# Regrouped weight loads and a moved row-moment step in a graph-attention kernel with fast matrix products

## The chip, the cores and the metric

The kernel runs on one core of one Trainium2 chip. The metric is the device time of one execution in microseconds. Before the change three runs gave a median of 3197.68 us (3193.69 to 3199.67). One execution was also recorded by the hardware profiler; all profile lines come from that one.

The names of the engines: PE is the matrix engine (PEld its weight loads), DVE the vector engine, ACT the scalar engine, POOL the GpSimd engine, SP the sync engine, whose queue (SPq) issues nearly all DMA transfers. Each engine runs its own instructions in order; engines wait for each other by semaphores.

## The reference

One attention layer over 128 graphs of 128 nodes, width 768, 12 heads of 64, all in float32:

```python
h = jnp.maximum(_layernorm(x, axis=-1), 0.0)
q = _split_heads(h @ Wq + bq); k = _split_heads(h @ Wk + bk); v = _split_heads(h @ Wv + bv)
scores = jnp.einsum('bhqd,bhkd->bhqk', q, k) / sqrt(64)
scores = jnp.where(adj > 0, scores + beta * adj, -9e15)
out = x + concat_heads(jnp.einsum('bhqk,bhkd->bhqd', softmax(scores), v))
```

x is (128, 128, 768), adj is (128, 128, 128) with some 12% of its entries above zero, and each of the three weight matrices is (768, 768), 2.36 MB.

## The kernel before, in words

Four graphs make a group `G` (512 rows); there are 32 groups. For each group the projections are done in three slices of equal size: `qk0` (the first half of the columns of q and k), `v`, and `qk1` (the second half of q and k). A slice is a matrix product of blocks, activations `A{r}{k}` by weights `B{k}{j}`, and is computed by a scheme of 15 block products instead of 18 (`PRODUCTS`): some factors are sums of activation blocks (`SUMS_A`, on DVE by `sum_acts`), some are sums of weight blocks (`SUMS_B`). In the slices `qk0` and `v` each of the 15 products is itself done by 7 products of quarters instead of 8 (`product_z`, line 486); that needs four more sums of each activation factor (`inner`, on POOL, L422 to L425, kept in the tiles `SP`), seven prepared quarters of each weight factor (`prepare`, made once at the start and kept in DRAM as `kept_qk` and `kept_v`), and a decoding on POOL (`decode`). The prepared weight tiles `T` of 448 KB are read back for each group by `load_T` (L301) into a ring of five (`RING`); the same five tiles serve `prepare` at the start. Each product issues the load of the tile five products later. The slice `qk1` uses plain products (`product`, L575) with its weights held on chip.

The first group is different: its `qk0` and `v` slices are plain (`plain_slice`, L780), and meanwhile `prepare` makes the 30 weight tiles from the raw weights: DVE makes the sums (L223, L225), POOL the quarters (L250 to L253, L276 to L279), SP sends the tile to DRAM (L255, L281). Group 1's statistics (`stats` L325, `moments_1` L336) stand inside group 0's `v` slice, on PE at its seventh product. The raw weights are loaded block by block by `load_weights`: `load_part` (L195) takes a block of 256 input rows in two DMAs of 128 rows each, and the DRAM side of such a DMA is a pattern of 4 by 32 rows (the kernel keeps its input rows in an order in which 32 neighbours lie together). The first three blocks are issued from SP and ACT, the rest from SP. The raw `qk0` and `v` blocks lie in the tiles that later hold `SP` (and, for the last three, `xo`), the `qk1` blocks in tiles of their own. SP's order at the start is: x of two graphs, first weights, x of the other two, the other `qk0` weights, adjacency and bias, `v` weights, `qk1` weights, first kept tile, x of group 1 (L165), the other kept tiles.

For groups from 3 on, the statistics of a group's rows are taken two groups ahead from copies of x (`load_halves` L370, `row_stats` L378), in the `qk1` slice. `row_moments` turns them into scale and shift: two instructions on DVE (L385, L387), two on POOL (L389, L390), then a small store to DRAM and a load back that spreads them over the partitions (L393, L394). `add_raw` loads the group's adjacency by four DMAs (L432); `bias_steps` turns it on DVE (L440) and makes the mask from it.

Attention is woven in between: `scores` (L613, L617, L620) for three heads pairs at a time, then `attend` places eight small steps between matrix products (`turn`). At the end of four of them `weigh` takes the row sums on DVE (L627, L628, L630) and ACT divides (L634). The result is added to x on POOL (`add`, L661) and stored (`send`, L664).

Inside the main loop the order of every engine's work is the order in which the program writes it. `run` (L748) is what writes it: for each product it issues the first half (matrix products, and the attention steps between them), then the functions that `todo` holds for this product (the fillers), then what `later` has put off for this product (`overdue`), then the second half (evacuation and accumulation of the product), then the functions held for "post". The steps of the change are in this order: in the loop over `G`, `row_moments` and `add_raw` for group `G + 1` are fillers of product 0 of the `qk0` slice.

Of the kernel before, what the change touches and what calls it, by code (L numbers as in the profile page):

```python
# [10 lines left out]
F32 = mybir.dt.float32  # L11
# [6 lines left out]
P = 128  # L18
HEADS = 12
GRP = 4  # L20
# [77 lines left out]

AS_SUMMED = ("B01", "B12", "B02", "B22", "B10", "B00", "B21", "B20", "B11")
SLICES = ("qk0", "v", "qk1")  # L100

# [15 lines left out]
def direct(ctx, tc, x, adj, wq, bq, wk, bk, wv, bv, beta, out, bad):  # L117
# [10 lines left out]
    nc = tc.nc  # L128
# [62 lines left out]

    def load_part(w, k, at, n, t, engine):
        src = w.rearrange("(a c j) n -> c a j n", a=NB, j=SQ)
        for c in range(2):
            engine.dma_start(t[:, c], src[2 * k + c][:, :, at:at + n])  # L195

    def load_block(sl, k, j, t, engines):
        if sl == "v":
            load_part(wv, k, j * 2 * P, 2 * P, t, engines[0])
        else:  # L200
            for i, w in enumerate((wq, wk)):
                load_part(w, k, (j + 3 * int(sl[2])) * P, P, t[:, :, i * P:(i + 1) * P], engines[i % len(engines)])

    nraw = [0]

    def load_weights(sl, blocks=[f"B{k}{j}" for j in range(3) for k in range(3)], engines=(nc.sync,)):
        for b in blocks:
            if sl == "qk1":
                t = const.tile([P, 2, H2], F32, name=f"{sl}_{HOME.get(b, b)}")
            else:  # L210
                n = nraw[0]
                nraw[0] += 1
                if n < len(PRODUCTS):
                    t = work.tile([P, GRP, P], F32, tag=f"SP{n}", name=f"{sl}_{b}", bufs=1)
                else:
                    t = work.tile([P, GRP, P], F32, tag="xo", name=f"{sl}_{b}", bufs=3)
                t = t.rearrange("p (c i) n -> p c (i n)", c=2)
            load_block(sl, int(b[1]), int(b[2]), t, engines)
            wt[sl, b] = t

# [6 lines left out]
    def sum_weights(sl, n):  # L227
        name, a, b, sign = SUMS_B[n]
        if (sl, name) not in wt:
            raw = [r for r, home in HOME.items() if home == name]  # L230
            wt[sl, name] = wt[sl, raw[0]] if raw else const.tile([P, 2, H2], F32, name=f"{sl}_{name}")
        sum_to(nc.vector, wt[sl, name], wt[sl, a.strip("-")], a[0] == "-", wt[sl, b], sign)
# [7 lines left out]
    def prepare(sl):  # L240

        def home(n):
            return work.tile([P, 7, P], F32, tag="T", name=f"prep_{sl}_{n}", bufs=RING)

        def whole(b):
            return wt[sl, b].rearrange("p c (i n) -> p c i n", i=2)

# [11 lines left out]
        def sums(name):  # L259
            for out, a, b, sign in SUMS_B:  # L260
                if out == name:
                    if out not in made:
                        made[out] = home(int(out[1:]))
                    at = [quarters(made[q]) if q in made else whole(q) for q in (a.strip("-"), b)]
                    sum_to(nc.vector, quarters(made[out]), at[0], a[0] == "-", at[1], sign)

        def finish(name):
            n = [i for i, p in enumerate(PRODUCTS) if p[1] == name][0]
            if name in made:
                rest(n, made[name])  # L270
            else:
                t, b = home(n), whole(name)
# [3 lines left out]
                e.tensor_tensor(t[:, 2], b[:, 1, 1], b[:, 0, 1], ALU.subtract)  # L276
# [141 lines left out]
    def inner(G, n):  # L418
        a = A[G, PRODUCTS[n][0]]
        t = SP[G, n] = work.tile([P, GRP, P], F32, tag=f"SP{ZORDER.index(n)}", name=f"SP{n}_{G}", bufs=1)  # L420
        e = nc.gpsimd
        e.tensor_tensor(t[:, 0], a[:, 0, N:H2], a[:, 1, N:H2], ALU.add)  # L422
# [33 lines left out]

    between, deferred = deque(), deque()

# [103 lines left out]
    def product(G, sl, n, order):  # L562
# [8 lines left out]
        for i in range(2):  # L571
            for c in range(2):
                lhs, rhs = b[:, c, i * P:(i + 1) * P], a[:, c, :]
# [67 lines left out]
    def attend_steps(G, oc):  # L641
        o = work.tile([P, 2, 4, HD], F32, tag="o", name=f"o_{G}_{oc}", bufs=2)
        for r in range(2):
            bank = take()
            pa = bank[:, 0:4 * VE].rearrange("p (b e) -> p b e", e=VE)
            for g in range(2):
                for i in range(2):
# [17 lines left out]

        later(add)
        later(send, 2)
        yield True
# [95 lines left out]
    def plain_slice(G, sl, todo):  # L764

        n = 0
        for r in range(2):
            for j in range(3):
# [4 lines left out]
                for at, k in [(at, k) for at in parts for k in range(3)]:  # L773
                    a, b = A[G, f"A{r}{k}"], wt[sl, f"B{k}{j}"]
                    for i in range(2):
                        for c in range(2):
                            lhs, rhs = b[:, c, i * P:(i + 1) * P], a[:, c, at]
                            if sl == "v":
                                lhs, rhs = a[:, c, i * N:(i + 1) * N], b[:, c, :]
                            last = nc.tensor.matmul(p[:, i, at], lhs, rhs, start=(k == 0 and i == 0 and c == 0),  # L780
# [170 lines left out]

    load_weights("qk1", AS_SUMMED)
    prep = deque(prepare("qk0") + prepare("v"))
# [44 lines left out]
    for G in range(1, NG):  # L998
# [41 lines left out]
        if G + 2 < NG:  # L1040
# [161 lines left out]
```

## Time and profile before

| | |
|---|---|
| median of 3 runs | 3197.68 us |
| the profiled execution | 3211.7 us, of which 3209.8 us span |
| mean granted clock of PE | 0.946 |
| busy: PE, DVE, ACT, POOL | 88%, 67%, 42%, 73% |
| DMA | 660.85 MB, mean 206 GB/s |
| one middle group | about 96.5 us |

The profile page lists busy time by engine, and then groups of instructions: line and engine, operation, output<-input by the program's names, partitions x elements, count, busy us, mean ns of one, and the idle time of the engine just before them with what ended it. A time line has one row for each run of equal instructions: start and duration in us, engine, line, operation, count, and in brackets the idle time before it and what ended that. For SPq the duration is that of issuing, with what it waited for between issues of one row. The waits list who waited for whom, with the total in us, the number of times and the longest. Windows give busy us of each engine in a stretch of time, then PE's granted clock, the mean busy share of the 16 DMA engines, and GB/s.

In a middle group the three slices stand at, for example, 983.5 to 1023.5 (`qk0`), 1023.5 to 1050.7 (`v`) and 1050.7 to about 1080 us (`qk1`); PE is busy 31.18 of 40.00 us, 26.56 of 27.20 and 29.30 of 29.30 in them.

### The profile page before, as it was taken

The numbers are of one execution on the slowest core, as the hardware profiler recorded it, in microseconds if no ns is written. First come the engines' busy times: TensorE is split into PE (matmuls) and PEld (weight loads), VectorE is DVE, ScalarE is ACT, GpSimd is POOL, SyncE is SP. The second block draws the span as 40 slices with busy tenths as digits, with TensorE's granted clock in tenths as the row PEclk, the third lists the DMA queues.
The fourth block names the chain that finished last, engine by engine and source line by source line (L and its number), as shares of the span: only waits on it lengthen the run. The fifth ranks groups of instructions, "written<-read, shape, count | busy, mean of one in ns | idle before, by whom it ended". The sixth has DMA issues, their size and how long they took to land.

```text
span 3209.8 us, 113028 instructions
## 1 busy us (share of the span) xinstructions
PE 2830.4 (88%) x46385; PEld 2462.4 (77%) x46385; DVE 2155.4 (67%) x4755; ACT 1338.4 (42%) x3999; POOL 2331.3 (73%) x4146
## 2 busy tenths in 40 slices
PE   7379988889888889888889888889888889888898
PEld 5267787778787778787778787778887778787787
DVE  3367666667666667667667667667666667666665
ACT  1134344344344344444344445344444344445343
POOL 2578677878777878767878677878777778677784
PEclk9689999999999999999999999999999999999999
DMA  3566776767776767776667776767776667776654
GB/s 95 172 184 186 235 227 206 207 196 215 233 225 206 207 193 211 237 221 201 205 195 221 238 221 202 206 195 218 239 230 203 201 194 217 237 222 202 199 186 146
DMA packets 531311, 660.85 MB, mean 206 GB/s; under 512 B 105181, under 2 KB 407529, under 8 KB 530793
## 3 DMA queue, kind: packets, MB, share of 16 engines
q1 hardware_dynamic: 529672, 652.81, 67.6%
q8 instruction: 367, 6.01, 0.8%
q14 instruction: 152, 1.24, 0.1%
q10 hardware_dynamic: 1120, 0.79, 0.1%
HBM read 589.26 MB, written 64.21 MB: 204 GB/s over the span
## 4 chain that ended last, share of the span: by engine, by line


## 5 line engine op out<-in xcount | busy, mean ns | idle before, releaser
L499 PE MATMUL bank<-SP,T_qk 128*64 128x128 f32 x7440 | 718.4, 287 | 0.2 <-issue 0.2
L499 PE MATMUL bank<-S,T_qk 128*64 128x128 f32 x4092 | 453.5, 295 | 255.2 <-DMA T_qk<-kept_qk 159.5
L499 PE MATMUL bank<-T_v,SP 128*64 128x128 f32 x7440 | 647.7, 273 | 0.0
L634 ACT ACTIVATE o<-bank,sm 128x64 f32<-128x64 f32 x1524 | 353.4, 315 | 679.0 <-DVE sm L628 583.6
L650 PEld LDWEIGHTS bank<-v,e 128*64 128x64 f32 x6048 | 427.2, 137 | 108.4 <-issue 1.0
L499 PEld LDWEIGHTS bank<-S,T_qk 128*64 128x64 f32 x4092 | 287.8, 150 | 279.3 <-DVE qk L526 136.8
L499 PEld LDWEIGHTS bank<-SP,T_qk 128*64 128x64 f32 x7440 | 496.5, 147 | 0.5 <-issue 0.5
L499 PEld LDWEIGHTS bank<-T_v,SP 128*64 128x64 f32 x7440 | 460.0, 137 | 0.0
L650 PE MATMUL bank<-v,e 128*64 128x65 f32 x6048 | 446.1, 221 | 0.9 <-issue 0.9
L575 PE MATMUL bank<-S,qk_T 128*64 128x256 f32 x3584 | 445.0, 381 | 0.0
L499 PE MATMUL bank<-T_v,S 128*64 128x128 f32 x4092 | 405.7, 274 | 18.8 <-ACT v L513 14.8
L585 ACT ACTIVATE qk<-bank,bqk 128x256 f32<-128x256 f32 x384 | 158.4, 475 | 569.5 <-PE bank L575 431.2
L544 POOL TENSOR_TENSOR qk<-qk 128x256 f32<-128x256 f32 x186 | 135.6, 729 | 357.2 <-DVE qk L525 357.2
L525 DVE TENSOR_TENSOR v<-v,bank 128x512 f32<-128x512 f32 x310 | 212.0, 684 | 156.9 <-PE bank L499 94.5
L575 PEld LDWEIGHTS bank<-S,qk_T 128*64 128x64 f32 x3584 | 235.5, 138 | 81.5 <-issue 2.2
L499 PEld LDWEIGHTS bank<-T_v,S 128*64 128x64 f32 x4092 | 260.1, 137 | 33.5 <-ACT v L513 23.9
L555 POOL TENSOR_TENSOR v<-v 128x128 f32<-128x128 f32 x186 | 85.5, 460 | 266.4 <-DVE v L525 172.1
L575 PE MATMUL bank<-S,qk_B 128*64 128x256 f32 x2048 | 276.0, 380 | 0.0
L525 DVE TENSOR_TENSOR qk<-qk,bank 128x512 f32<-128x512 f32 x310 | 209.3, 675 | 98.7 <-PE bank L499 97.4
L661 POOL TENSOR_TENSOR xo<-xo,o 128x512 f32<-128x512 f32 x189 | 254.6, 1347 | 11.7 <-ACT o L634 11.7
L617 DVE SCALAR_TENSOR_TENSOR e<-bank,biasT 128x512 f32<-128x512 f32 x378 | 236.5, 681 | 28.1 <-PE bank L613 27.0
L575 PE MATMUL bank<-A,qk_T 128*64 128x256 f32 x2048 | 249.1, 379 | 0.0
(157 smaller groups left out, 5882.5 us busy)
## 6 DMA issues: line engine op xcount, KB each, us to landing
T_qk<-kept_qk SPq DMA_DIRECT2D x465, 448.0 KB
T_v<-kept_v SPq DMA_DIRECT2D x465, 448.0 KB
x<-in_x_dram SPq DMA_DIRECT2D x254, 192.0 KB
xo<-in_x_dram SPq DMA_DIRECT2D x189, 256.0 KB
out_dram<-xo SPq DMA_DIRECT2D x189, 256.0 KB
half<-in_x_dram SPq DMA_DIRECT2D x232, 192.0 KB
adj<-in_adj_dram SPq DMA_DIRECT2D x128, 64.0 KB
kept_qk<-prep_qk SPq DMA_DIRECT2D x15, 448.0 KB
```

Source lines behind the costliest of these rows:

```text
L499: nc.tensor.matmul(p[z // 4][q:q + HD, z % 4, :], lhs[:, q:q + HD], rhs, start=(first and z % 4 == 0), stop=True, skip_group_check=True)
L525: nc.vector.tensor_tensor(t[:, 0:4], t[:, 0:4], p[0], op)
L544: e.tensor_tensor(t[:, 1:4:2], t[:, 1:4:2], twice(0), ALU.add)
L555: e.tensor_tensor(v[:, 0:2, 0:HD], heads(0), heads(3), ALU.add)
L575: nc.tensor.matmul(p[q:q + HD, i, :], lhs[:, q:q + HD], rhs, start=(first and i == 0 and c == 0), stop=(c == 1), skip_group_check=True)
L585: opened[0] = nc.scalar.activation(t[:, i, :], p[:, i, :], AF.Identity, bias=bqk[:, i, oc:oc + 1], scale=float(sign))
L617: taken[0] = nc.vector.scalar_tensor_tensor(e, ps[oc, i].rearrange("p (g n) -> p g n", g=GRP), SCORE_CAP * ISCALE, biasT[G], op0=ALU.min, ...
L634: nc.scalar.activation(o[:, b], pa[:, b, 0:HD], AF.Copy, scale=t[:, 1, b:b + 1])
L650: nc.tensor.matmul(pa[q:q + HD, 2 * g + i, :], es[G, oc, i][:, 2 * r + g, q:q + HD], vt[G, "v", r, h // 4][:, 4 * g + h % 4, :], start=Tru ...
L661: nc.gpsimd.tensor_add(t, t, o.rearrange("p a (b j) d -> p (a b) (j d)", j=2))
```

## The change

Four things are done at once.

Weights: the raw weights of a slice are loaded into one large tile. A DMA takes 32 input rows (one value of `a`) with all six chunks of rows (`c`) and 128 to 512 columns; q and k of `qk0` in two parts (first column block, then the other two), `v` in one part of 512 columns and three small tiles for the last 256, `qk1` in one part. All are issued from SP. The blocks `B{k}{j}` are views of the large tiles.

Sums: the 15 `SP` tiles become slots of one tile, `spbuf`, which also holds the raw `qk0` and `v` weights at the start. Because of it the first group's DVE order differs: its 11 activation sums stand ahead of the first weight sums, where they alternated.

Moments and adjacency: `row_moments` and `add_raw` move from product 0 of a group's `qk0` slice to product 14 of the `qk1` slice before it, behind the other fillers there.

Row sums: `weigh` and the release of its bank are put off until the fillers of the same product have been issued (`weighing`); the add and the store of an attention result move one product later.

The lines of the profile of the changed kernel are shifted by 2 or 3, for example L393 becomes L395 and L301 becomes L303.

```diff
-    def load_part(w, k, at, n, t, engine):
-        src = w.rearrange("(a c j) n -> c a j n", a=NB, j=SQ)
-        for c in range(2):
-            engine.dma_start(t[:, c], src[2 * k + c][:, :, at:at + n])
...
+    spbuf = const.tile([P, len(PRODUCTS), GRP, P], F32, name="spbuf")
+    rows_of = {}
+    for name, w in (("q", wq), ("k", wk), ("v", wv)):
+        rows_of[name] = w.rearrange("(a c j) n -> a j c n", a=NB, j=SQ)
+
+    def load_cols(engine, t, name, at, chunks=slice(0, NC)):
+        for a in range(NB):
+            engine.dma_start(t[a * SQ:(a + 1) * SQ], rows_of[name][a][:, chunks, at:at + t.shape[-1]])
+
+    def flat(lo, hi):
+        return spbuf[:, lo:hi].rearrange("p s g n -> p (s g n)")
+
+    def raw_qk(u, t, parts):
+
+        v = t.rearrange("p (c i j n) -> p c i j n", c=NC, i=2, j=3)
+        for lo, hi in parts:
+            for i, name in enumerate(("q", "k")):
+                load_cols(nc.sync, v[:, :, i, lo:hi].rearrange("p c j n -> p c (j n)"), name, (lo + 3 * u) * P)
+        for k in range(3):
+            for j in range(3):
+                wt[f"qk{u}", f"B{k}{j}"] = v[:, 2 * k:2 * k + 2, :, j]
+
+    def raw_v():
+        t = flat(9, 15).rearrange("p (c n) -> p c n", c=NC)
+        load_cols(nc.sync, t, "v", 0)
+        for k in range(3):
+            own = work.tile([P, GRP, P], F32, tag="xo", name=f"v_B{k}2", bufs=3)
+            own = own.rearrange("p (c i) n -> p c (i n)", c=2)
+            load_cols(nc.sync, own, "v", 4 * P, slice(2 * k, 2 * k + 2))
+            for j in range(3):
+                b = t[:, 2 * k:2 * k + 2, j * 2 * P:(j + 1) * 2 * P] if j < 2 else own
+                wt["v", f"B{k}{j}"] = b.rearrange("p c (i n) -> p c i n", i=2)
...
-    load_weights("qk0", ["B00", "B10", "B20"], (nc.sync, nc.scalar))
+    raw_qk(0, flat(0, 9), ((0, 1),))
     load_x(0, 1)
-    load_weights("qk0", [f"B{k}{j}" for j in range(1, 3) for k in range(3)])
+    raw_qk(0, flat(0, 9), ((1, 3),))
...
-        t = SP[G, n] = work.tile([P, GRP, P], F32, tag=f"SP{ZORDER.index(n)}", name=f"SP{n}_{G}", bufs=1)
+        t = SP[G, n] = spbuf[:, ZORDER.index(n)]
...
                     if g == i == 1:
-                        weigh(G, oc, r, pa, o[:, r])()
-                        give(bank)
+                        weighing.append(lambda r=r, pa=pa, bank=bank: (weigh(G, oc, r, pa, o[:, r])(), give(bank)))
...
-        later(add)
-        later(send, 2)
+        later(add, 2)
+        later(send, 3)
...
             for f in todo.get(at, ()):
                 f()
+            while weighing:
+                weighing.popleft()()
             overdue()
...
-    load_weights("v", AS_SUMMED)
+    raw_v()
...
-    load_weights("qk1", AS_SUMMED)
+    raw_qk(1, const.tile([P, NC * VH * 2], F32, name="wqk1"), ((0, 3),))
...
         elif more:
-            then(0, row_moments, G + 1)
-            then(0, add_raw, G + 1)
             bias(G + 1, 3, 5, 6, 12)
...
             for r, at in enumerate((6, 11)):
                 then(at, load_x, G + 2, r)
+            then(14, row_moments, G + 2)
+            then(14, add_raw, G + 2)
         slice_of(G, "qk1", todo)
```

More of the change, by code (lines that the diff above doesn't have):

```diff
@@ L97 @@
 HOME = {"B00": "T12", "B10": "T10", "B02": "T0", "B20": "T4", "B11": "T13"}
-AS_SUMMED = ("B01", "B12", "B02", "B22", "B10", "B00", "B21", "B20", "B11")
-SLICES = ("qk0", "v", "qk1")
 SC_AT = 1
@@ L190, in direct @@
     wt = {}
-    def load_part(w, k, at, n, t, engine):
-        src = w.rearrange("(a c j) n -> c a j n", a=NB, j=SQ)
-        for c in range(2):
-            engine.dma_start(t[:, c], src[2 * k + c][:, :, at:at + n])
[L197 to L219, printed above, removed]
+    spbuf = const.tile([P, len(PRODUCTS), GRP, P], F32, name="spbuf")
@@ L230, in sum_weights @@
             raw = [r for r, home in HOME.items() if home == name]
-            wt[sl, name] = wt[sl, raw[0]] if raw else const.tile([P, 2, H2], F32, name=f"{sl}_{name}")
+            if raw:
+                wt[sl, name] = wt[sl, raw[0]]
+            else:
+                wt[sl, name] = const.tile([P, 2, 2, P], F32, name=f"{sl}_{name}")
         sum_to(nc.vector, wt[sl, name], wt[sl, a.strip("-")], a[0] == "-", wt[sl, b], sign)
@@ L243, in home @@
             return work.tile([P, 7, P], F32, tag="T", name=f"prep_{sl}_{n}", bufs=RING)
-        def whole(b):
-            return wt[sl, b].rearrange("p c (i n) -> p c i n", i=2)
         def rest(n, t):
@@ L263, in sums @@
                         made[out] = home(int(out[1:]))
-                    at = [quarters(made[q]) if q in made else whole(q) for q in (a.strip("-"), b)]
+                    at = [quarters(made[q]) if q in made else wt[sl, q] for q in (a.strip("-"), b)]
                     sum_to(nc.vector, quarters(made[out]), at[0], a[0] == "-", at[1], sign)
@@ L271, in finish @@
             else:
-                t, b = home(n), whole(name)
+                t, b = home(n), wt[sl, name]
                 e = nc.gpsimd
@@ L455, in direct @@
     banks, added, opened = {}, {}, {}
-    between, deferred = deque(), deque()
+    between, deferred, weighing = deque(), deque(), deque()
     def later(f, slots=1):
@@ L572, in product @@
             for c in range(2):
-                lhs, rhs = b[:, c, i * P:(i + 1) * P], a[:, c, :]
+                lhs, rhs = b[:, c, i], a[:, c, :]
                 for q in range(0, P, HD):
@@ L776, in plain_slice @@
                         for c in range(2):
-                            lhs, rhs = b[:, c, i * P:(i + 1) * P], a[:, c, at]
+                            lhs, rhs = b[:, c, i], a[:, c, at]
                             if sl == "v":
-                                lhs, rhs = a[:, c, i * N:(i + 1) * N], b[:, c, :]
+                                lhs, rhs = a[:, c, i * N:(i + 1) * N], b[:, c].rearrange("p i n -> p (i n)")
                             last = nc.tensor.matmul(p[:, i, at], lhs, rhs, start=(k == 0 and i == 0 and c == 0),
```

## The prediction

> **What bounds the kernel now.** I read the page's busy shares first, then the groups with their idle time, then the waits of PE and of the SP queue, then the time line of one middle group on PE, SP and POOL, and last the windows and time lines of the first 180 us.
>
> The page: PE is busy 88% of the span and its idle time is concentrated. Of 380 us idle, 255.2 us stand before one group, the qk products whose weights come from DRAM.
>
> ```profile
> PE 2830.4 (88%) x46385; PEld 2462.4 (77%) x46385; DVE 2155.4 (67%) x4755; ACT 1338.4 (42%) x3999; POOL 2331.3 (73%) x4146
> ...
> L499 PE MATMUL bank<-S,T_qk 128*64 128x128 f32 x4092 | 453.5, 295 | 255.2 <-DMA T_qk<-kept_qk 159.5
> ```
>
> The waits of the SP queue (engine, line, what it waited for, total us, times, longest):
>
> ```profile
> SPq L393 <- POOL SP L422: 117.2, 29, 4.2
> SPq L394 <- DMA turned<-row: 38.1, 29, 1.3
> ```
>
> The time lines of one group, first PE, then SP, then POOL:
>
> ```profile
> 997.08 0.44 PE L499 MATMUL bank<-S,T_qk 128*64 128x128 f32 x4 [2.52 <-DMA T_qk<-kept_qk]
> ...
> 1005.12 0.69 PE L499 MATMUL bank<-S,T_qk 128*64 128x128 f32 x4 [6.29 <-DVE qk L526]
> ```
>
> ```profile
> 984.15 8.40 SPq L664 DMA_DIRECT2D out_dram<-xo  x2
> 992.64 0.46 SPq L301 DMA_DIRECT2D T_qk<-kept_qk  x1
> 996.95 0.57 SPq L393 DMA_DIRECT2D turned<-row  x1
> 998.91 0.52 SPq L394 DMA_DIRECT2D block<-turned  x1
> 999.52 2.02 SPq L432 DMA_DIRECT2D adj<-in_adj_dram  x4
> 1001.64 0.43 SPq L301 DMA_DIRECT2D T_qk<-kept_qk  x1
> ```
>
> ```profile
> 990.85 1.27 POOL L661 TENSOR_TENSOR xo<-xo,o 128x512 f32<-128x512 f32 x1
> ...
> 995.63 1.01 POOL L389 TENSOR_TENSOR row<-verow,nhalf 128x4 f32<-128x4 f32 x1
> 996.73 0.20 POOL L390 TENSOR_TENSOR row<-meanrow,row 128x4 f32<-128x4 f32 x1
> ```
>
> The reader should see that both PE gaps of a group hang on the SP queue, and that queue on POOL. PE finishes the fifth product of the qk0 slice at 994.5. The sixth weight tile was issued at 992.64, behind a store that waited for POOL's add (ended 992.12); it served PE at 997.08. The seventh was issued at 1001.64, behind L393, which waited for POOL's L390 to end at 996.93 (the table of waits names L422, which ran just after), behind L394, which waited for L393's landing, and behind four adjacency loads; it served PE at 1005.12. DVE names itself there (L526) only because it stood behind the transpose of the adjacency, which landed at the same time. The offsets repeat in every group I looked at: seventh tile issued 4.7 us after L393, used 3.3 to 3.9 us later; sixth used 3.6 to 4.4 us after issue. The two gaps make 255.2/30 = 8.5 us a group. POOL is a backlog here, not idle: it runs without a break from early in the qk1 slice to 998.7, 15 us after PE has left that slice (983.5).
>
> The beginning, in windows (us from the start; PE, PEld, DVE, ACT and POOL busy, granted clock, DMA share, GB/s), and on the time lines of SP, POOL and PE:
>
> ```profile
> 80.00:98.00 18.00, 0.00 (x0) 0.00 (x0) 0.00 (x0) 0.00 (x0) 0.00 (x0) 0.61 0.29 83
> 104.00:112.00 8.00, 0.00 (x0) 0.00 (x0) 1.14 (x4) 0.74 (x5) 1.83 (x5) 0.50 1.09 293
> ```
>
> ```profile
> 97.95 0.61 SPq L255 DMA_DIRECT2D kept_qk<-prep_qk  x1
> ```
>
> ```profile
> 103.80 0.45 POOL L276 TENSOR_TENSOR prep_qk<-qk_B 128x128 f32<-128x128 f32 x1 [48.66 <-DMA kept_qk<-prep_qk]
> ...
> 176.54 1.00 POOL L916 TENSOR_TENSOR bv_b<-bv_b 128x384 f32<-128x384 f32 x1
> ```
>
> ```profile
> 130.29 0.43 PE L336 MATMUL bank<-st,mean 128*64 128x32 f32 x4 [51.29 <-DVE st L325]
> ```
>
> From 80 to 98 us no engine works: the weights trickle in at 83 GB/s, and behind them in the same queue stand the first kept tile (97.95) and group 1's x. POOL, whose ring of five prepared tiles is full at 55, resumes at 103.80; PE waits 51.29 us. When the x tiles go out (32 rows by 8 pieces a DMA), the same queue moves 293 GB/s.
>
> **The change, part by part.**
>
> *Weight loads.* Before, 90 DMAs of 64 or 128 KB (4.6 MB of q and k, 2.4 MB of v); after, 16 for qk0, 16 for v, 8 for qk1, with the shape of the x loads. At 83 GB/s the 7.1 MB take 85 us; at the x loads' 232 to 293 GB/s, 24 to 30 us. So all raw weights are in by about 35 to 45 us, and the kept tiles and group 1's x no longer queue.
> Whether few engines or few bytes in flight made the 83 GB/s, the trace leaves open: the share of 0.29 fits either. The Trainium skill, page "DMA: Bandwidth & Descriptors", section "Why a DMA increments its semaphore by 16 and not by 1", says that a DMA uses the largest number up to 16 that divides the slowest dimension of both patterns; here that would be 4 before and 16 after, so an estimate of four times 83 GB/s. If instead the limit were the bytes in flight (the program makes each DMA wait for the one eight before it), the first DMAs' 96 KB for 64 would give 1.5 times, and qk0's 2.4 MB would take 19 us instead of 7; POOL would then start a few us later. By the one the sum stays, by the other it loses up to 10 us.
>
> What then sets the end of the beginning is POOL's preparation of 30 tiles: PE's first scores (finished at 175.5, after 14 us of waits for DVE's L792) need a sum that stands on DVE among sums that wait for POOL's ring, and the next group's work follows POOL. Before: first five tiles 39.81 to 55.14 (15.3 us), pause, 25 tiles from 103.80 to 176.54 (72.7, of which 6.0 idle). After: PE's first product no longer waits until 16.99 for ACT (blocked in issuing six weight loads), about 7 us earlier; so DVE's transposes end at 31 instead of 38.3. But all 11 activation sums now stand ahead of the first weight sum (before, one by one between them): 11 x 0.60 (their spacing) + 0.7, POOL starts at 38.6. First five tiles: between 1.94 us (the tile at 53.20) and 3.07 each; without DVE's interleaved sums 2.2, so 11. Then 66.7 without the 6.0 idle: 116.3. Gain 60. Lower end, POOL as slow as before and the 6 us kept: 39.8 + 15.3 + 72.7 = 127.8, gain 49. Upper end, every tile 1.94: POOL ends at 97, then PE's own v slice (38 us of products after qk0 ends near 50, plus some 10 for moments) holds its scores until 101 instead of 173.6, gain 72. I take 58, since DVE must still wait for group 1's x. Cover for the 7 us at PE's start: POOL's chain, so not added.
>
> *Row moments and adjacency, 29 times.* Moved from product 0 of the qk0 slice to product 14 of the qk1 slice before. On DVE, L385 and L387 (0.42 + 0.16) move ahead of two accumulations: nothing, since POOL takes L389 8 us later. On POOL the pair stays behind the same inner sums; only the add of the third attention (1.27) now falls behind it. So L390 ends 1.27 earlier. On SP the six DMAs (L393, L394, four L432) now stand ahead of the sixth weight tile and the third store. With L393's old start as zero: chain starts at -1.27, sixth tile issued 4.69 later at +3.42, used 3.3 to 4.4 later at +6.7 to +7.8, take 7.0 (3.6, where the two ranges meet). PE's fifth product ended at -2.3 (994.5 against 996.95, likewise elsewhere). One gap of 9.3 us (9.0 to 10.1) replaces two of 8.5 together. Seventh to tenth tiles follow at once, and PE takes them slower than they come (0.43 us of issue each against 1.75 us a product). Half clock after the gap (four matmuls 0.69 instead of 0.39, for 3.5 us) comes once in both. So +0.8 a group, bounds -0.5 (if POOL reaches the pair 1.4 us earlier) and +1.6: 29 x 0.8 = +23 us, from -15 to +46.
>
> *Row sums behind the fillers.* L627, L628, L630 (0.16 + 0.18 + 0.36) go behind the DVE sums of the same product and still ahead of its accumulations. Queued behind them: ACT's four divides, POOL's add, the bank. A row-statistics filler can wait for its DMA (L378: 106.6 us in 35 waits), now with the row sums behind it. PE has no gap in the qk1 slice (29.30 busy of 29.30 from 1050.7), DVE is busy 21.65 there, so nothing; with the cover gone 0.7 us for each of six, 4 us a group. Adds and stores one slot later: the store's wait for POOL on SP shortens, and T loads behind it have 5 us to spare. Nothing.
>
> *One tile for sums, large weight tiles.* Same instructions; each matmul waits for the sums of its own slot. Nothing; a false wait would show as a PE gap at product 1.
>
> **Sum.** -58 + 23 = -35 us against the profiled execution's 3211.7 (span 3209.8 and 1.9 around it), which is 0.44% above the median of 3197.68. As a share 1.09%, so 3163.
>
> **Rivals.**
> 1. The middle gets what the move aims at: adjacency and T tiles early, second gap gone. 29 x 6.3 = 183, so 3197.7 - 58 - 183 = 2957. Against it: the chain cannot start before POOL's pair, which stays behind the backlog. A milder form, POOL 2 us earlier and 1 us a group gained: 3111.
> 2. Beginning gains half, because DVE's wait for group 1's moments holds POOL's ring: -28 + 23, 3193.
> 3. Slower: the sixth tile waits longer behind the chain. If the add's removal brings nothing and the tile needs 4.4 us, it is used at 4.69 + 4.4 = 9.1, the gap is 11.4, +2.9 a group, +84: 3224. It decides from 2.0 us a group (58/29). For it: six DMAs pass ahead of a tile that used to be early. Against: after L432 the seventh tile took 3.3 to 3.9.
> 4. The loads stay at 83 GB/s (nothing gained at the start): 3221. Against: the x loads' 232 to 293.
>
> **Chances.** Forecast 0.55 (own range 3111 to 3195: -87 to -3); rival 1 strong 0.04, mild 0.10; rival 2 0.13; rival 3 0.14; rival 4 0.04. Under 0.2% (6 us) a measurement cannot tell from no change. Rival 2 splits between faster and same; forecast's upper edge gives a little to same. Faster 0.75, same 0.09, slower 0.16. The range takes in rival 2 and the mild rival 1 and reaches towards rival 3: 3108 to 3206.
>
> **What would show it.** Right: DMA share above 0.6 while weights load, first kept tile near 42 us, PE's gap at L336 under 15 us, POOL's L916 near 116; in each middle group one gap of about 9 us at the sixth product, released by a T tile, and no second one. Wrong: two gaps again, a gap over 11 us, POOL waiting in its preparation, or PE waiting in the qk1 slice.

## The result, and the profile after

The changed kernel takes 3173.59 us (median of 3 runs, 3171.12 to 3177.0) against 3197.68: ratio 0.9928, 95% interval 0.9905 to 0.995. A second comparison gave 3172.56 against 3202.73: 0.9909 (0.9894 to 0.9924). So it is 24 to 30 us faster; 35 were forecast. One execution of all those below, of the kernel with consecutive weight rows, took 4254.43 us at a granted clock of 0.618 and is left out of its ratio.

The page of the kernel after, busy time and the group that held most of PE's idle time (last part of a line: idle time before the group and what ended most of it):

```profile
PE 2807.9 (89%) x46385; PEld 2452.2 (77%) x46385; DVE 2163.9 (68%) x4755; ACT 1341.2 (42%) x3999; POOL 2323.2 (73%) x4146
...
L501 PE MATMUL bank<-S,T_qk 128*64 128x128 f32 x4092 | 443.5, 292 | 289.5 <-DMA T_qk<-kept_qk 288.7
```

The same group as before, and its idle time grew, from 255.2 to 289.5 us, by 34.3/29 = 1.2 us a group. What ended it is now a weight tile's DMA nearly throughout (288.7 us); before, part was put down to DVE. The gain must lie elsewhere.

The waits of the SP queue after (engine, line, what it waited for; total us, times, longest):

```profile
SPq L395 <- POOL row L392: 242.1, 29, 8.4
SPq L396 <- DMA turned<-row: 39.2, 29, 1.7
```

One middle group after: PE, then SP, then POOL (start, duration, engine, line, operation, count, and idle time before with its releaser):

```profile
1049.88 0.69 PE L501 MATMUL bank<-S,T_qk 128*64 128x128 f32 x4 [9.30 <-DMA T_qk<-kept_qk]
```

```profile
1041.21 0.55 SPq L395 DMA_DIRECT2D turned<-row  x1
1043.17 0.52 SPq L396 DMA_DIRECT2D block<-turned  x1
1043.78 2.02 SPq L434 DMA_DIRECT2D adj<-in_adj_dram  x4
1045.89 0.43 SPq L303 DMA_DIRECT2D T_qk<-kept_qk  x1
1046.43 0.40 SPq L665 DMA_DIRECT2D out_dram<-xo  x1
```

```profile
1039.89 1.02 POOL L391 TENSOR_TENSOR row<-verow,nhalf 128x4 f32<-128x4 f32 x1
1040.98 0.20 POOL L392 TENSOR_TENSOR row<-meanrow,row 128x4 f32<-128x4 f32 x1
1041.13 1.26 POOL L662 TENSOR_TENSOR xo<-xo,o 128x512 f32<-128x512 f32 x1
```

One gap instead of two. The sixth weight tile goes out 1045.89 - 1041.21 = 4.68 us after the chain's first DMA, which starts when POOL's pair has ended, and PE has it 3.99 us later. POOL's add of the third attention (L662) now stands behind the pair.

The beginning after, in windows (us from the start; PE, PEld, DVE, ACT and POOL busy, granted clock, DMA share, GB/s), then SP, POOL and PE:

```profile
0.00:20.00 20.00, 14.59 (x95) 13.38 (x95) 8.25 (x28) 4.35 (x11) 2.74 (x19) 0.91 0.89 187
20.00:40.00 20.00, 13.10 (x53) 11.06 (x51) 12.45 (x22) 4.20 (x11) 6.30 (x6) 0.74 0.97 193
```

```profile
40.16 0.36 SPq L257 DMA_DIRECT2D kept_qk<-prep_qk  x1
```

```profile
50.51 0.46 POOL L278 TENSOR_TENSOR prep_qk<-spbuf 128x128 f32<-128x128 f32 x1 [2.92 <-DMA kept_qk<-prep_qk]
...
57.23 0.45 POOL L280 TENSOR_TENSOR prep_qk<-prep_qk 128x128 f32<-128x128 f32 x1 [5.85 <-ACT prep_qk L277]
...
60.13 0.46 POOL L278 TENSOR_TENSOR prep_qk<-spbuf 128x128 f32<-128x128 f32 x1 [1.92 <-DMA kept_qk<-prep_qk]
...
125.25 1.01 POOL L919 TENSOR_TENSOR bv_b<-bv_b 128x384 f32<-128x384 f32 x1
```

```profile
78.55 0.43 PE L338 MATMUL bank<-st,mean 128*64 128x32 f32 x4 [10.83 <-DVE st L327]
```

The stretch without any work (80 to 98 us) is gone. The DMA share is 0.89 and 0.97 while the weights come, the first kept tile goes out at 40.16 instead of 97.95, and POOL ends its preparation at 125.25 instead of 176.54: 51.3 us earlier.

The two profiled executions differ by 38.0 us of span. 51.3 from the beginning, less 34.3 lost to the gaps, plus 22.5 by which PE's busy time is smaller, come to 39.5. Of the last, 9 to 15 us are that one execution's and not the change's: the profile of before had 2830.4 us of busy PE, and the four kernels below with the same matmuls and at most one part of the change (loads alone, row sums alone, move alone, consecutive rows) had 2815.0, 2819.3, 2821.3 and 2820.1. The other 7 to 13 us seem to come with the change (four more runs that hold all or most of it had 2803.3 to 2812.2); where they come from was not followed.

### The profile page after: what moved, and what is told of

The parts are those of the page before. It is cut to its first block, busy times and chain, and to the rows that moved or that the text cites. A ratio compares the mean times of both kernels' runs of the same rounds, so it can differ in the third digit from the quotient of the medians.

```text
span 3171.8 us, 113085 instructions
## 1 busy us (share of the span) xinstructions
PE 2807.9 (89%) x46385; PEld 2452.2 (77%) x46385; DVE 2163.9 (68%) x4755; ACT 1341.2 (42%) x3999; POOL 2323.2 (73%) x4146
## 4 chain that ended last, share of the span: by engine, by line
## 5 line engine op out<-in xcount | busy, mean ns | idle before, releaser
L501 PE MATMUL bank<-spbuf,T_qk 128*64 128x128 f32 x7440 | 707.0, 285 | 0.9 <-issue 0.9
L501 PE MATMUL bank<-S,T_qk 128*64 128x128 f32 x4092 | 443.5, 292 | 289.5 <-DMA T_qk<-kept_qk 288.7
L501 PE MATMUL bank<-T_v,spbuf 128*64 128x128 f32 x7440 | 648.5, 273 | 1.3 <-issue 1.3
L501 PEld LDWEIGHTS bank<-spbuf,T_qk 128*64 128x64 f32 x7440 | 484.6, 146 | 1.0 <-issue 1.0
L501 PEld LDWEIGHTS bank<-T_v,spbuf 128*64 128x64 f32 x7440 | 459.4, 137 | 1.4 <-issue 1.4
L577 PE MATMUL bank<-S,wqk 128*64 128x256 f32 x3072 | 402.4, 380 | 0.0
L577 PE MATMUL bank<-S,qk_T 128*64 128x256 f32 x2560 | 317.1, 381 | 0.0
L520 ACT ACTIVATE qk<-bank,bqk 128x128 f32<-128x128 f32 x186 | 67.7, 364 | 438.5 <-PE bank L501 379.0
L662 POOL TENSOR_TENSOR xo<-xo,o 128x512 f32<-128x512 f32 x189 | 242.0, 1280 | 11.8 <-ACT o L636 11.6
L622 ACT ACTIVATE e<-e 128x512 f32<-128x512 f32 x378 | 223.8, 633 | 8.9 <-DVE e L619 8.8
```

Source lines behind the costliest of these rows:

```text
L501: nc.tensor.matmul(p[z // 4][q:q + HD, z % 4, :], lhs[:, q:q + HD], rhs, start=(first and z % 4 == 0), stop=True, skip_group_check=True)
L520: nc.scalar.activation(t[:, 0], p[0][:, 0], AF.Identity, bias=bqk[:, 0, oc:oc + 1], scale=float(sign))
L622: nc.scalar.activation(e, e, AF.Exp, scale=1.0 / ISCALE)
L662: nc.gpsimd.tensor_add(t, t, o.rearrange("p a (b j) d -> p (a b) (j d)", j=2))
```

## The experiments

Ratios are to the kernel before on the same chip, with 95% intervals. Six runs undo or isolate parts of the change, one repeats it, and five go on along its cause.

### Parts of the change by themselves

**The weight loads alone**: the kernel after with everything else put back.

```
-            then(14, row_moments, G + 2)
-            then(14, add_raw, G + 2)
...
+            then(0, row_moments, G + 1)
+            then(0, add_raw, G + 1)
...
-        later(add, 2)
-        later(send, 3)
+        later(add)
+        later(send, 2)
```

> The kernel before with the new weight loads and the one tile of sums alone; row moments, adjacency, row sums, adds and stores stand where they stood. Theory (the gain of the beginning, 51.3 us in the trace of after, arrives whole at the end): 3197.7 - 51 = 3146, POOL's last piece of preparation ends near 125, and each middle group keeps its two gaps of 8.5 us together. Rival (the groups behind become slower because of the beginning or of the large tiles, for example by transfers that now meet): about as fast as the kernel after, 3174, and the gaps of a middle group are not those of before.

Measured: 3152.39 against 3203.84, ratio 0.9867 (0.9829 to 0.9904): 51.5 us by the medians. Its page and its POOL time line:

```profile
L501 PE MATMUL bank<-S,T_qk 128*64 128x128 f32 x4092 | 444.5, 293 | 254.4 <-DMA T_qk<-kept_qk 155.2
```

```profile
125.92 1.01 POOL L920 TENSOR_TENSOR bv_b<-bv_b 128x384 f32<-128x384 f32 x1
```

POOL ends its preparation as early as in the kernel after, and the gaps are those of before (254.4 us). The four runs lie between 3142.47 and 3177.26 us, so the size is not sharp: 43 us by the ratio, 31 to 55 by its interval, which takes in the 51 expected. The loads alone beat the whole change, and everything else in it costs: 21 to 27 us by the medians, 13 to 20 by the ratios. The gaps themselves differ by 35.1 us (289.5 and 254.4); PE's busy time makes good 7.1 of it (2815.0 and 2807.9), the rest was not followed.

**Row sums, adds and stores later, alone.**

```
-                        weigh(G, oc, r, pa, o[:, r])()
-                        give(bank)
+                        weighing.append(lambda r=r, pa=pa, bank=bank: (weigh(G, oc, r, pa, o[:, r])(), give(bank)))
...
-        later(add)
-        later(send, 2)
+        later(add, 2)
+        later(send, 3)
```

> The kernel before with the row sums behind the fillers, the attention's add one slot later and its store one slot later, nothing else. What the prediction put on these: nothing, 3198. Theory formed from the order of the two queues: on POOL the third add still stands ahead of the row moments, so the chain starts as before; on SP the sixth weight tile passes the third store (its gap of 2.5 us goes), and the store now stands between the adjacency loads and the seventh tile, which is issued 0.5 us later. So one gap of 8.5 to 9.0 us instead of two that make 8.5: 0 to +0.5 us a group, 3198 to 3212.

Measured: 3231.75 against 3203.84, ratio 1.009 (1.0071 to 1.0109): slower by 28 us, more than either expectation. The group with the gaps, and its share of waits for tiles:

```profile
L499 PE MATMUL bank<-S,T_qk 128*64 128x128 f32 x4092 | 443.1, 293 | 287.0 <-DMA T_qk<-kept_qk 247.9
```

The direction and place are those expected from the order of the queues: one gap, at the seventh tile, which is issued 5.23 us after the chain starts (4.7 before), because the store now stands between. The size is not: 287.0 - 255.2 = 31.8 us, 1.1 a group for 0.5. The single gaps of the 29 groups are 9.0 to 10.5 us long.

**The move alone**: row moments and adjacency loads at product 14 of the slice before.

```
-            then(0, row_moments, G + 1)
-            then(0, add_raw, G + 1)
...
+            then(14, row_moments, G + 2)
+            then(14, add_raw, G + 2)
```

> The kernel before with the row moments and the adjacency loads moved to the last product of the slice before, nothing else. Theory A (the gain of 1.27 us in the chain's start comes from the add that falls behind the pair on POOL, and this happens only because the add is also a slot later): here the add stays ahead, the chain starts as before, the sixth tile is issued behind the chain and the third store, 4.69 + 0.5 us after the chain's start, and used 3.3 to 4.4 us later at about +8.8; PE has stood since -2.3, so the gap is 11.1 us instead of 8.5: +2.6 a group, 29 times, 3198 + 75 = 3273. Theory B (the move brings what the kernel after shows, whatever the adds do): +0.5 to +1.2 a group, 3212 to 3232.

Measured: 3283.67 against 3203.84, ratio 1.0247 (1.022 to 1.0273), 80 us slower: theory A.

```profile
L499 PE MATMUL bank<-S,T_qk 128*64 128x128 f32 x4092 | 445.4, 293 | 341.2 <-DMA T_qk<-kept_qk 341.2
```

341.2 - 255.2 = 86 us, 3.0 a group (2.6 expected). The sixth tile goes out 5.2 us after the chain's start, behind the six DMAs and the store, and PE has waited 10.95 to 12.74 us. Alone the parts cost 80 and 28 us, together 13 to 27: one of the later edits makes the move bearable.

**Which of the two later edits does that**: the kernel after with the row sums at their old place, adds and stores still later.

```
-                        weighing.append(lambda r=r, pa=pa, bank=bank: (weigh(G, oc, r, pa, o[:, r])(), give(bank)))
+                        weigh(G, oc, r, pa, o[:, r])()
+                        give(bank)
```

> The kernel after with the row sums back at their old place, ahead of the fillers of the product; the adds and stores stay one slot later. Theory (in the combination it is the add's and the store's slot that the move needs, and the place of the row sums costs and brings nothing): ratio 0.991 as after, gaps of 9.65 us a group. Rival (the row sums behind the fillers bring part of it, because ACT's divides and POOL's add get their inputs at another time): the add comes earlier or later on POOL, the chain's start moves against PE, and the time differs by over 0.3%.

Measured: 3186.59 against 3201.69, ratio 0.9949 (0.9936 to 0.9962), against 0.9909 for the kernel after on the same chip: the rival, by 0.4%, some 13 us (from the first comparison, 0.9928, it is not apart: the intervals overlap). The gaps are 297.0 us, where the move alone had 341.2 and the kernel after has 289.5: so it is mostly the slot that the add and the store give up that makes the move bearable. DVE's waits in the kernel after, and then in this one:

```profile
DVE sm L629 <- PE bank L652: 114.3, 168, 1.5
```

```profile
DVE sm L629 <- PE bank L652: 162.7, 206, 2.5
```

With the row sums ahead of the fillers DVE waits 48 us longer for PE's attention products, the fillers (activation sums that POOL needs) behind them. A group lasts 97.4 us instead of 96.8 (starts of the chain 18 groups apart), of which the gaps explain less than half (297.0 us for 289.5). How the rest comes about was not followed.

**The kernel after again**, on the chip of the two runs that change the bias and the qk1 weights below.

> The kernel after itself, on the same chip as the two runs beside it: ratio 0.993 to before, 9.65 us of gap a group.

Measured: 3172.56 against 3202.73, 0.9909 (0.9894 to 0.9924), with 289.4 us of gaps.

### Why the loads were slow

**The kernel before, each weight load's 128 rows read consecutively.** Number, size, tiles and queues of the 90 loads stay.

```
-        src = w.rearrange("(a c j) n -> c a j n", a=NB, j=SQ)
+        src = w.rearrange("(c p) n -> c p n", p=P)
         for c in range(2):
-            engine.dma_start(t[:, c], src[2 * k + c][:, :, at:at + n])
+            engine.dma_start(t[:, c], src[2 * k + c][:, at:at + n])
```

> The kernel before, whose 90 weight loads keep their number, size, tiles and queues; only the 128 rows of each are read as consecutive rows of the weight matrix instead of four runs of 32 rows that lie 192 rows apart. The weights therefore stand in another order of rows and the output is not the reference's; every instruction's work is the same. If the rate of 83 GB/s came from the form of the loads (four outer pieces, so few engines take part): the rate rises to that of the x loads, 230 GB/s or more, POOL's preparation ends 40 to 60 us earlier and the time is 3140 to 3160. If it came from the bytes in flight (64 and 128 KB a load, eight loads open): nothing changes, 3198.

Measured: 3150.63 to 3168.37 against 3203.84, ratio 0.9863 (0.9826 to 0.99): 44 us, as good as the new loads alone by their ratio (0.9867). SP's 18 loads of the v weights, first in the kernel before, then here, and where POOL's preparation ends here:

```profile
42.25 24.09 SPq L195 DMA_DIRECT2D v_B<-in_L_gnn_Wv_dram  x18
```

```profile
25.96 9.26 SPq L195 DMA_DIRECT2D v_B<-in_L_gnn_Wv_dram  x18
...
130.55 1.00 POOL L916 TENSOR_TENSOR bv_b<-bv_b 128x384 f32<-128x384 f32 x1
```

18 loads of 128 KB issued in 24.09 us are 98 GB/s, in 9.26 us 255. The windows say the same: 97 GB/s at a DMA share of 0.32 before (42 to 66 us), 257 at 0.91 here (26 to 35 us). It was the form of the load, not its size nor the number of bytes in flight: the rival explanation that the prediction left open is out.

The Trainium skill (page "DMA: Bandwidth & Descriptors", section "Why a DMA increments its semaphore by 16 and not by 1") has a DMA use as many engines as the largest number up to 16 that divides the slowest dimension of both patterns, here 4 and then 16. The trace does not show the number of engines; the shares of 0.32 and 0.91 agree with it.

The run changes two things at once, the outer dimension (4 to 128) and the distance of the rows (runs of 32 that lie 192 apart, then neighbours). That rows lie apart does not by itself slow a load: the x loads of the prediction, with an outer dimension of 32, step over rows that lie 32 apart and ran at 293 GB/s. No run changed the outer dimension alone.

POOL still ends 4.6 us later than with the large loads (130.55 and 125.92). The number of issues is the likely reason: SP needs 9.26/18 = 0.51 us a load here, and while it issues the 64 KB loads behind them at about 0.45 us each (35 to 45 us) the DMA share is only 0.56.

### Why the beginning gave 51 and not 58

**The kernel after with the 8 loads of the qk1 weights behind group 1's x.**

```
-    raw_qk(1, const.tile([P, NC * VH * 2], F32, name="wqk1"), ((0, 3),))
+    wqk1 = const.tile([P, NC * VH * 2], F32, name="wqk1")
...
         then(6, load_x, 1, r)
+    then(8, raw_qk, 1, wqk1, ((0, 3),))
```

> The kernel after with the 8 loads of the qk1 weights (2.4 MB) issued behind group 1's x instead of ahead of it and of the first kept tile. Theory (POOL's ring of five tiles waits, some 11 us in the beginning, because the kept tiles and group 1's x stand behind the last weight loads in the queue and share the DMA engines with them): POOL's last piece of preparation ends 4 to 8 us earlier, near 119, and the time is 3166 to 3170. Rival (the ring waits for DVE's statistics of group 1 and for the kept tiles' own transfers): no change, 125 and 3174.

Measured: 3173.81 against 3172.56 for the kernel after on the same chip: no change. Its POOL in the preparation:

```profile
56.64 0.46 POOL L280 TENSOR_TENSOR prep_qk<-prep_qk 128x128 f32<-128x128 f32 x1 [9.43 <-ACT prep_qk L277]
64.18 0.46 POOL L278 TENSOR_TENSOR prep_qk<-spbuf 128x128 f32<-128x128 f32 x1 [4.67 <-DMA kept_qk<-prep_qk]
```

DVE gets group 1's x 8.2 us earlier (its statistics start at 46.57 instead of 54.77), but POOL now waits 14.1 us in the ring instead of 10.7, since the qk1 weights pass most of the kept tiles, and ends at 127.34. My theory that the place of these loads holds the ring falls. Group 1's x, the qk1 weights and the kept tiles share the DMA engines there, whose mean share in the kernel after is 1.08 from 40 to 50 us and 0.99 from 50 to 65, and either order tried makes one of the three late. That fewer bytes there would help was not tried.

### Whose gap it is

**The pair two products earlier**: the kernel after with 12 in place of 14.

```
-            then(14, row_moments, G + 2)
-            then(14, add_raw, G + 2)
+            then(12, row_moments, G + 2)
+            then(12, add_raw, G + 2)
```

> The kernel after with row moments and adjacency loads at product 12 of the qk1 slice instead of 14, right behind the last row statistic; on POOL the pair then stands ahead of three inner sums (12 operations of some 0.46 us, 5.5 us). Theory (POOL's backlog alone sets when the chain starts, and the chain alone sets the gap): the chain starts 5.5 us earlier, the sixth tile is used at +2.9 on the old scale instead of +8.4 to +8.9, the seventh, behind the third store, at about +5.4: each gap of 9.65 shrinks to about 4.5 us, 29 times 5, 3174 - 145 = 3029 (3010 to 3050). Rival (POOL is not what holds the pair: DVE's row statistic and the loads in front of it hold it): less than 2 us a group, 3116 or more.

Measured: 3038.33 against 3208.63, ratio 0.947 (0.9454 to 0.9486); 140 us below the kernel after by the ratios (0.9909 - 0.947 of 3200), 145 expected.

```profile
L501 PE MATMUL bank<-S,T_qk 128*64 128x128 f32 x4092 | 444.2, 292 | 160.7 <-DMA T_qk<-kept_qk 155.8
```

The gaps fall by 128.8 us, 4.4 a group. So POOL's order sets when the chain starts; the rival, which allowed less than 2 us a group, is out. The tile still waits behind the chain (issued 5.2 to 6.7 us after it).

**The chain behind the tiles**: pair, turned row and adjacency at product 5 of the qk0 slice, and the bias steps, which use the adjacency, at products 9, 10, 11 and 13.

```
-            then(14, row_moments, G + 2)
-            then(14, add_raw, G + 2)
...
-            bias(G + 1, 3, 5, 6, 12)
+            then(5, row_moments, G + 1)
+            then(5, add_raw, G + 1)
+            bias(G + 1, 9, 10, 11, 13)
```

> The kernel after with row moments and adjacency loads at product 5 of the qk0 slice, behind the weight tiles six to eleven, and the four steps of the bias at products 9, 10, 11 and 13 instead of 3, 5, 6 and 12. Theory (the gap is the place of the chain's six DMAs ahead of the sixth tile): the sixth tile goes out as soon as its slot is free, no gap there; next in line is the third store, which waits for POOL's add until about +0.1 and stands ahead of the seventh tile: used at about +4.6, when PE has stood since +0.8. A gap of 3.8 us instead of 9.65, 3174 - 170 = 3004 (2985 to 3030). Rival (the gap is POOL's lateness, and only moves with the chain to where the chain is): 3174 or slower.

Measured: 3136.68 against 3208.63, ratio 0.9782 (0.9765 to 0.9798): far from 3004. PE's waits, then SP's wait inside the chain:

```profile
PE bank L501 <- DMA T_qk<-kept_qk: 109.9, 38, 4.1
PE bank L652 <- ACT o L636: 72.8, 29, 4.9
```

```profile
SPq L396 <- DMA turned<-row: 169.6, 29, 7.1
```

The gap at the seventh tile is 3.0 to 4.1 us a group where 3.8 was expected. What I had not counted: behind the small DMA of the turned row, which is issued after a burst of five 448 KB tiles, the queue waits 5.8 us (169.6/29) instead of 1.4, so the adjacency is late; DVE's transpose waits for it, the row sums stand behind the transpose, the bank behind the row sums, and PE's attention waits 72.8 us. (That this wait comes by way of the transpose is shown two runs below, where the bias moves and it goes.) PE's busy time is also 37 us longer than in the kernel after (2844.5); why was not followed.

**Stores behind the tiles as well.**

```
-        later(send, 3)
+        later(send, 7)
```

> The same kernel as the one with the chain behind the tiles, with each attention's store four slots later still (seven instead of three), so that the third store too stands behind five more weight tiles. Theory: nothing that waits for POOL stands ahead of a weight tile any more, the gaps of 9.65 us go nearly whole (0 to 1 us stays at the twelfth tile, which stands behind the chain): 29 times 8.6 to 9.65, 3174 - 250 to 280 = 2894 to 2924, and up to 45 us less if the half clock behind each gap goes too (four matmuls at 0.69 instead of 0.39 us for some 3.5 us: about 1.5 us a group). Rival (POOL's backlog shows up elsewhere, as a wait of PE for inner sums or of DVE for accumulators): no better than the kernel with the chain alone behind the tiles, about 3004.

Measured: 3013.0 against 3208.63, ratio 0.9395 (0.9379 to 0.941). 124 us below the chain alone behind the tiles, so the rival falls; but 90 to 120 short of the theory.

```profile
PE bank L652 <- ACT o L636: 107.5, 29, 4.8
...
PE bank L501 <- DMA T_qk<-kept_qk: 3.1, 6, 0.9
```

```profile
1099.21 0.71 DVE L442 STREAM_TRANSPOSE adjT<-adj 128x512 f32<-128x512 f32 x1 [4.36 <-DMA adj<-in_adj_dram]
```

The waits for qk weight tiles are gone: 288.7 to 3.1 us. The wait of 3.7 us a group for the bank took part of their place.

**The bias later too**, at products 12, 13, 14 and 8 of the v slice.

```
-            bias(G + 1, 9, 10, 11, 13)
+            bias(G + 1, 12, 13, 14)
...
+            else:
+                bias(G + 1, 8)
```

> The kernel with the chain and the stores behind the tiles, and besides the four steps of the bias at products 12, 13 and 14 of the qk0 slice and 8 of the v slice (instead of 9, 10, 11 and 13). Theory (its one wait of 107.5 us on PE, at the attention's matmuls, comes from DVE's transpose of the adjacency, which waits 4.4 us for its loads with the row sums, and so the bank, behind it): 3013 - 107 = 2906 (2890 to 2925), the wait at the attention's matmuls below 15 us in all. Rival (the bank is late because ACT's divides or POOL's add are late by themselves): above 2960.

Measured: 3020.57 against 3202.73, ratio 0.9438 (0.9409 to 0.9467): no gain. The named wait is gone, as expected, and another of the same size has come up close by, before the twelfth product. PE, then SP in one group:

```profile
PE bank L501 <- DMA T_qk<-kept_qk: 106.7, 40, 4.6
```

```profile
1005.79 0.56 SPq L395 DMA_DIRECT2D turned<-row  x1
1009.56 0.53 SPq L396 DMA_DIRECT2D block<-turned  x1
1010.18 2.02 SPq L434 DMA_DIRECT2D adj<-in_adj_dram  x4
1012.30 0.43 SPq L303 DMA_DIRECT2D T_qk<-kept_qk  x1
```

SP stands 6.5 us in the chain, and the twelfth tile behind it comes late. In the previous run PE's wait for the bank, just ahead of it, had hidden that.

**The chain cut in two**: the second half goes behind three more tiles.

```
+    def row_back(G):
+
+        to, turned = rows[G, "to"]
         nc.sync.dma_start(to.rearrange("p b s g -> p (b s g)"),
...
             then(5, row_moments, G + 1)
-            then(5, add_raw, G + 1)
+            then(8, row_back, G + 1)
+            then(8, add_raw, G + 1)
```

> The kernel with chain, stores and bias later, and the chain cut in two: the pair on POOL and the first DMA of the turned row stay at product 5, the second DMA, which waits for the first one's landing (3.2 us here), and the four adjacency loads go to product 8, behind three more weight tiles. Theory (in the kernel with the bias later the wait of 107 us moved to the twelfth tile, because the queue stands 6.5 us in the chain: 3.2 us of them for the landing): no tile stands behind a landing any more, the waits of PE for weight tiles fall from 106.7 to below 15 us, 3020 - 95 = 2925 (2905 to 2940). Rival (the weight tiles themselves come too slowly once PE does not pause, 448 KB every 1.75 us = 262 GB/s, so any order leaves such a wait): above 2980.

Measured: 2922.46 against 3203.3, ratio 0.9124 (0.9099 to 0.9149), as expected (2925). It beats both kernels.

```profile
PE 2764.6 (95%) x46385; PEld 2397.2 (82%) x46385; DVE 2194.7 (75%) x4755; ACT 1344.0 (46%) x3999; POOL 2339.5 (80%) x4146
```

```profile
PE bank L506 <- DMA T_v<-kept_v: 37.6, 33, 3.1
...
PE bank L506 <- DMA T_qk<-kept_qk: 17.3, 23, 1.9
```

PE's waits for weight tiles are 54.9 us instead of 292.6 (288.7 and 3.9 in the kernel after). The time is the one expected, but only in part for the reason given: the waits were to fall below 15 us and fell to 54.9, with 37.6 of them now at the v tiles. Against the previous run the span is 94 us shorter (3016.2 and 2922.0); 40.5 of that is PE's busy time (2805.1 and 2764.6), at a granted clock of 0.990 for 0.974, which the expectation did not count. POOL does the same work as there, in the same order but for the pair and the bias: its backlog was not the bound, only what it kept waiting in SP's queue.

## Why the prediction was right, and where it was off

The time was forecast at 3163 and came at 3173.6, inside the range and inside the likeliest case's own range. The mechanism of both terms was right; how near the number came is partly luck. By the traces the beginning brought 51.3 us for 58, and the gaps cost 34.3 for 23: together 17 us gained where 35 were forecast. The measured 24 to 30 is reached with PE's busy time, 7 to 13 us below that of the kernels with at most one part of the change, which no term held.

- **Weight loads: right.** Forecast were a DMA share above 0.6 (0.89 and 0.97), raw weights in by 35 to 45 us (last load issued by 39.9), first kept tile near 42 (40.16), the gap of PE ahead of the moments under 15 us (10.83). Rival 4 (the rate stays) is out, and the contiguous rows show why: the form of the load.
- **Gain of the beginning: mis-sized, 58 against 51.3.** Here a step of the working failed. The sum set POOL's start at 38.6; it came 3.2 us earlier (35.41). It took the ring's 6.0 us of waiting away; 10.7 us were there (2.92 + 5.85 + 1.92). 116.3 - 3.2 + 10.7 = 123.8, and the trace shows 125.25; the rest is the first five tiles, 12.2 us (35.41 to 47.59) for 11. They fill the ring before the queue is free, as they did before, only for 10.7 us instead of 54.7. The waiting was taken for an effect of the slow weight loads in front; the kept tiles wait for their transfers beside other bytes too, in windows in which the DMA share is 0.99 and 1.08. The run with the qk1 weights later shows that their place alone does not change it.
- **Row chain: right, and for the reason given, its price too low.** One gap of 9.3 us (9.0 to 10.1) was forecast; 289.5/30 = 9.65. The chain's start moved ahead because the third add falls behind the pair, the sixth tile went out 4.68 us after the chain's start where 4.69 was worked out, and its time to use was 3.7 to 4.3 us where 3.6 was taken. In the gaps the term of +23 us came as 34.3, 1.2 us a group for 0.8; in the time, the kernel after against the loads alone, as 13 to 27. No second gap, no milder form of rival 1; rival 3's mechanism is there with 1.2 us a group instead of 2.9, short of the 2.0 from which it decides.
- **"Nothing" for the row sums, adds and stores one slot later: wrong as terms, harmless in the sum.** The prediction booked the add's passing under the move. By themselves these edits cost 28 us, the move alone 80, and both together 13 to 27; within the pair, the place of the row sums is worth some 13. The prediction asked what waits behind the moved instructions, but not what each edit would do without the other: which of chain, store and sixth tile stands ahead on SP.
- **One tile for sums, large weight tiles: nothing, right.** With the loads alone the gaps are 254.4 us, and no new wait stands in the middle.
- **The base of the sum.** The profiled execution of before lay 14 us above its median, and the forecast scaled it by a share. By the traces 9 to 15 of PE's 22.5 us less are that execution's own, so it was right not to take 3211.7 as the base.

## What to carry to other kernels

Read a gap by the queue that the late transfer stands in, and then by what stands ahead of it there: all six DMAs of the chain, which serve the next group, stood ahead of a tile that PE needed at once, and moving them and the stores behind the tiles, and cutting the chain in two, brought some ten times what this change brought (the chain's move alone, without the rest, some 40 us). Parts that reorder the same queue have no price of their own; cost them together and in each order, and after every wait that is taken away, ask which one it had hidden (here three in a row). For strided loads, compare one with a neighbour of the same size and another outer dimension before blaming size or queue depth.

## What the runs showed that I had not expected

- A small DMA's landing goes with what was issued just ahead of it: behind the turned row (some 4 KB) the queue waits 1.3 us before and 1.4 after, 2.9 and 3.0 us after spaced tiles (84.4/29 and 87.3/29), 5.8 us after a burst of tiles. In one group the DMA share in the two microseconds from the chain's start is 0.04 before and after, 0.82 and 0.59 after spaced tiles, 0.99 after the burst.
- The granted clock goes with the gaps: mean 0.926 with the move alone (341.2 us of gaps), 0.946 in the kernel after, 0.990 where the gaps are nearly gone, and PE's busy time is 43 us less (2807.9 to 2764.6) for the same matmuls: a sixth of that kernel's lead of 250 us over the kernel after.
- The v loads' rate rose from 98 to 255 GB/s with nothing changed but which rows a load reads.
